# Householder steps of a 64x64 eigensolver beside a graph layer: explicit reflector products in place of a replicated rank-two update

## The chip, the cores and the metric

The kernel runs on one core of one Trainium2 chip. The metric is the device time of one execution in microseconds (us). A comparison is made from the medians of several runs; the profile shows one execution.

## The reference

Four graph layers follow each other, each ending in `x = layernorm(x + layer(x))`, over `x` of 128 batches, 64 nodes and 256 features, with one 64x64 matrix `adj`. All is float32.

```python
# layer 0
def slconv(x, adj, S, W):
    return einsum('nm,bmh->bnh', adj * S, einsum('bnf,fh->bnh', x, W))   # S is adj here
h = relu(slconv(x, adj, adj, W1)); h = relu(slconv(h, adj, adj, W2)); out = slconv(h, adj, adj, W3)

# layer 1
deg = sum(A, 0) + sum(A, 1) - diagonal(A); d = where(deg > 0, rsqrt(deg), 0)
_, U = eigh(d[:, None] * (diag(deg) - A) * d[None, :])
h = relu(einsum('mn,bnd->bmd', U.T, x) @ W1 + b1); out = einsum('nm,bmd->bnd', U, h @ W2 + b2)

# layer 2: two graph convolutions, then four LSTMs over windows of 1 to 4 nodes
# layer 3: x @ W + b_lin, scores masked by adj, softmax over the 64 nodes, sum of neighbours
```

What matters here is that layer 1 needs the eigenvectors `U` of a 64x64 matrix that depends on `adj` alone. So they can be computed while layer 0 runs.

## The kernel before

**Part one** is layer 0 together with the eigenvectors. The 8192 rows (batch times node) lie in `X` as 64 tiles of 128 rows. `layer0(g)` takes two tiles, for g from 0 to 31: mixing over nodes with `sqT2` (the squared, transposed matrix of two batches on the diagonal), the product with `aw1`, ReLU, mixing, the product with `aw2`, ReLU, the product with `aw3`, mixing, then an addition to `X` on VectorE (L626) and `rows_norm`, whose statistics run on VectorE, whose power runs on GpSimd (L452, L453) and whose last step runs on VectorE (L455). ScalarE moves the results from PSUM, as ReLU (L584) or copy (L595, L622). Five PSUM buffers (`psa`) serve layer 0.

`eigen()` computes the eigenvectors in these stages: the normalised Laplacian; 62 Householder steps to a tridiagonal matrix, which also collect the transformation in `QT`; the eigenvalues by six passes of a bisection with 16 points each (L272 to L289, VectorE alone); the eigenvectors of the tridiagonal matrix by recurrences from both ends (L302 to L304) and a choice of signs; then `U` and its transpose for two batches, `u2` and `ut2`. `eigen()` has three PSUM tags of one buffer each: `pa`, `pb`, `pc`. All its products go through one helper (L75), and all products of layer 0 and later go through another (L576), so their lines in the profile are these two; the tile names tell the products apart.

**The Householder step before.** The matrix and `QT` stand side by side in one tile `AQ` of 128 partitions, of which the upper 64 are zero in their constants. A step has two products, issued one after the other. The first, with the vector `v` broadcast as weights, gives `v` times the matrix and `v` times `QT` in all 128 partitions; the second fetches the next row, by a unit vector. Everything else is some 24 small VectorE instructions on rows and columns: the length of the vector, one square root on ScalarE (L145), the coefficients, and the rank-two update of `AQ` in place (L174 to L176).

**What sets the order.** Inside part one TensorE's instructions are recorded by hand. `layer0(g)` and `eigen()` are generators. Each `yield` returns the estimated time at which its next products may be issued; a loop at the end of part one picks `eigen()` if it is due, else the first of two running layer-0 groups. The clock `now` is advanced by stated costs: in layer 0 by `2 * max(0.0009 * columns, 0.112)` us per product, in `eigen()` by 0.2 us. `eigen()` states its own due times with

```python
    def after(n, turns=0):
        clock[0] += 0.21 * n + 0.6 * turns
        return clock[0] + 0.3
```

where `n` counts VectorE instructions. The other engines' orders are set by the framework's scheduler. Every engine works off its queue in order, so a TensorE product that waits for VectorE holds up all products behind it.

**Part two** is layers 1 to 3, over 16 groups of four tiles, three at a time, with an order of its own. Layer 1 needs `u2` and `ut2`, and starts when layer 0's last group is through. The change does not touch it.

Of the kernel before, what the change touches and what calls it, by code (L numbers as in the profile page):

```python
# [10 lines left out]
F32 = mybir.dt.float32  # L11
AF = mybir.ActivationFunctionType
ALU = mybir.AluOpType
AX = mybir.AxisListType

N = 64
FAN = 16
PASSES = 6
CONSTS = ["eye", "rev", "sup", "sub", "ones", "off", "idx"]


def constants():
    k = np.arange(N)
    eye = np.eye(N)
    sup = np.eye(N, k=1)
    c = {
        "eye": eye,
        "ones": np.ones((N, N)),
        "rev": eye[::-1],
        "sup": sup,  # L30
        "sub": sup.T,
        "off": 1 - eye,
        "idx": np.tile(k, (N, 1)),
    }
    out = np.zeros((2 * N, len(CONSTS), N), np.float32)
    out[:N] = np.stack([c[n] for n in CONSTS], axis=1)
    return out


def eigen(tc, stack, a, cst, u2, ut2, now):  # L40
# [9 lines left out]
    V, S, PE = nc.vector, nc.scalar, nc.tensor  # L50
    cp = stack.enter_context(tc.tile_pool(name="ec", bufs=1))
# [4 lines left out]
    def sb(shape, tag):  # L56
        uid[0] += 1
        return wp.tile(shape, F32, tag=tag, name=f"{tag}_{uid[0]}")

    def ps(shape, tag):  # L60
        uid[0] += 1
        return pp.tile(shape, F32, tag=tag, name=f"{tag}_{uid[0]}")

    W = 2 * N
    C = {n: cst[:N, i, :] for i, n in enumerate(CONSTS)}
    eye = cst[:, CONSTS.index("eye"), :]
    clock = [now[0]]

    def after(n, turns=0):

        clock[0] += 0.21 * n + 0.6 * turns
        return clock[0] + 0.3

    def mm(out, lhsT, rhs):
        PE.matmul(out, lhsT, rhs, start=True, stop=True)  # L75
        now[0] += 0.2
        clock[0] = now[0] + 0.5

    def rowdot(out, x, y):
        junk = sb([N, N], "junk")  # L80
        V.scalar_tensor_tensor(junk, x, 1.0, y, op0=ALU.mult, op1=ALU.mult, accum_out=out)


    aT = ps([N, N], "pa")
    PE.transpose(aT, a, C["eye"])
    s2 = sb([N, N], "s2")
    V.tensor_add(s2, a, aT)
    dia = sb([N, 1], "c0")
    rowdot(dia, a, C["eye"])
    deg = sb([N, 1], "c1")  # L90
# [6 lines left out]
    y = sb([N, 1], "c4")  # L97
# [11 lines left out]
    V.tensor_scalar(m, s2, -0.5, None, op0=ALU.mult)  # L109
    V.tensor_mul(m, m, C["off"])  # L110
    V.scalar_tensor_tensor(m, C["eye"], dl, m, op0=ALU.mult, op1=ALU.add)
    dm = sb([N, N], "dm")
    V.tensor_scalar(dm, C["eye"], y, None, op0=ALU.mult)
    pm = ps([N, N], "pa")
    yield after(20, 1)
    mm(pm, m, dm)

    AQ = cp.tile([W, 2, N], F32, name="AQ")
    V.memset(AQ[:, 0, :], 0.0)
    V.tensor_copy(AQ[:, 1, :], eye)  # L120
    V.tensor_scalar(AQ[:N, 0, :], pm, y, None, op0=ALU.mult)
    A, QT = AQ[:N, 0, :], AQ[:N, 1, :]
    yield after(3)

    pq = ps([W, 3, N], "pc")
    mm(pq[:, 2, :], eye[:, 0:1].to_broadcast([W, W]), AQ[:, 0, :])  # L130
    xr = sb([W, N], "xr")
    V.tensor_copy(xr, pq[:, 2, :])
    after(1)
    for i in range(N - 2):
        j = i + 1
        q = sb([W, 16], "q")
        rest, rm, ss, sq, g0, sg, rc, n2, vv, th, s0, c2, qi = (q[:, k:k + 1] for k in range(13))
        u = sb([W, 4], "u")
        v, vt, pt, qt = (u[:, k:k + 1] for k in range(4))
        v0 = xr[:, j:j + 1]  # L140
        V.scalar_tensor_tensor(sb([W, N], "junk")[:, j + 1:], xr[:, j + 1:], 1.0, xr[:, j + 1:], op0=ALU.mult,
                               op1=ALU.mult, accum_out=rest)
        V.tensor_scalar(rm, rest, 1e-30, None, op0=ALU.add)
        V.tensor_scalar(ss, v0, v0, rm, op0=ALU.mult, op1=ALU.add)
        S.activation(sq, ss, AF.Sqrt)  # L145
        V.tensor_scalar(g0, rest, 0.0, -1.0, op0=ALU.is_gt, op1=ALU.mult)
        V.tensor_scalar(sg, v0, 0.0, 0.5, op0=ALU.is_ge, op1=ALU.subtract)
        V.reciprocal(rc, sq)
        V.tensor_scalar(n2, ss, rc, sq, op0=ALU.mult, op1=ALU.add)
        V.scalar_tensor_tensor(v0, n2, sg, v0, op0=ALU.mult, op1=ALU.add)  # L150
        V.scalar_tensor_tensor(sb([W, N], "junk")[:, j:], xr[:, j:], 1.0, eye[:, j:], op0=ALU.mult, op1=ALU.mult,
                               accum_out=v)
        yield after(21, 0.5)
        pq = ps([W, 3, N], "pc")
        mm(pq[:, 0:2, :], v.to_broadcast([W, W]), AQ)
        mm(pq[:, 2, :], eye[:, j:j + 1].to_broadcast([W, W]), AQ[:, 0, :])
        V.tensor_scalar(vv, v0, v0, rm, op0=ALU.mult, op1=ALU.add)
        V.reciprocal(vv, vv)
        V.tensor_mul(th, vv, g0)
        V.tensor_scalar(s0, v0, th, 2.0, op0=ALU.mult, op1=ALU.mult)  # L160
        V.tensor_scalar(vt, v, th, 2.0, op0=ALU.mult, op1=ALU.mult)
        V.scalar_tensor_tensor(sb([W, N], "junk")[:, j:], AQ[:, 0, j:], 1.0, xr[:, j:], op0=ALU.mult, op1=ALU.mult,
                               accum_out=pt)
        V.tensor_scalar(pt, pt, th, 2.0, op0=ALU.mult, op1=ALU.mult)
        V.scalar_tensor_tensor(sb([W, N], "junk")[:, j:], pq[:, 0, j:], th, xr[:, j:], op0=ALU.mult, op1=ALU.mult,
                               accum_out=c2)
        qr = sb([W, N], "qr")
        V.scalar_tensor_tensor(qr[:, j:], xr[:, j:], c2, pq[:, 0, j:], op0=ALU.mult, op1=ALU.add)
        V.tensor_scalar(qi, qr[:, j:j + 1], th, 2.0, op0=ALU.mult, op1=ALU.mult)
        nx = sb([W, N], "xr")  # L170
        V.scalar_tensor_tensor(nx[:, j + 1:], qr[:, j + 1:], s0, pq[:, 2, j + 1:], op0=ALU.mult, op1=ALU.add)
        V.scalar_tensor_tensor(nx[:, j + 1:], xr[:, j + 1:], qi, nx[:, j + 1:], op0=ALU.mult, op1=ALU.add)
        V.scalar_tensor_tensor(qt, vt, c2, pt, op0=ALU.mult, op1=ALU.add)
        V.scalar_tensor_tensor(AQ[:, 0, j:], qr[:, j:], vt, AQ[:, 0, j:], op0=ALU.mult, op1=ALU.add)  # L174
        V.scalar_tensor_tensor(AQ[:, 0, j:], xr[:, j:], qt, AQ[:, 0, j:], op0=ALU.mult, op1=ALU.add)
        V.scalar_tensor_tensor(AQ[:, 1, :], pq[:, 1, :], vt, AQ[:, 1, :], op0=ALU.mult, op1=ALU.add)  # L176
        xr = nx


    de = cp.tile([N, 4], F32, name="de")  # L180
    d, e, ep, g = (de[:, j:j + 1] for j in range(4))
    rowdot(d, A, C["eye"])
    rowdot(e, A, C["sup"])
# [19 lines left out]
    def rows(col, n, tag):  # L203
        b = sb([N, N], "bc")
        V.tensor_scalar(b, C["ones"], col, None, op0=ALU.mult)
        yield after(5)
        p = ps([N, n, N], tag)
        mm(p, b, cst[:N, 0:n, :])
        return p

    co = cp.tile([N, 20], F32, name="co")
# [13 lines left out]
    t0, t1, t2, big, ae, sg = w_[11:17]  # L225
# [45 lines left out]
    for _ in range(PASSES):  # L271
        V.tensor_scalar(h, h, 1.0 / (FAN + 1), None, op0=ALU.mult)  # L272
        x = sb([N, FAN], "bx")
# [3 lines left out]
        for k in range(1, N):  # L277
# [3 lines left out]
            if k % 2:  # L281
                yield after(5)
        V.scalar_tensor_tensor(M.rearrange("p j k -> p k j"), Q, 0.0, inb.unsqueeze(2).to_broadcast([N, N, FAN]),
                               op0=ALU.is_lt, op1=ALU.mult)
# [3 lines left out]
                               accum_out=co_[6])  # L288
# [10 lines left out]
    for k in range(1, N):  # L299
        c = N - 1 - k  # L300
# [35 lines left out]
    Z = cp.tile([N, N], F32, name="Z")  # L336
# [76 lines left out]

    yield after(16)
    pu = ps([N, N], "pa")
    mm(pu, Z, QT)
    UT = cp.tile([N, N], F32, name="UT")
    V.tensor_scalar(UT, pu, co_[12], None, op0=ALU.mult)
    yield after(1)
    pt = ps([N, N], "pb")  # L420
# [15 lines left out]
P = 128  # L436
# [23 lines left out]
def kernel(  # L460
# [26 lines left out]
    V, S, PE = nc.vector, nc.scalar, nc.tensor  # L487
# [5 lines left out]
    def tl(pool, shape, tag):  # L493
        uid[0] += 1
        return pool.tile(shape, F32, tag=tag, name=f"{tag}_{uid[0]}")
# [7 lines left out]
    pa = phase_a.enter_context(tc.tile_pool(name="pa", bufs=2))  # L503
    ea = phase_a.enter_context(tc.tile_pool(name="ea", bufs=1))
# [9 lines left out]
    nc.gpsimd.memset(ad2, 0.0)  # L514
    adst = keep.tile([P, N], F32, name="adst")
    a64 = ea.tile([N, N], F32, name="a64")
    eig_c = ea.tile([P, len(CONSTS), N], F32, name="eig_c")
    nc.sync.dma_start(a64, adj)
    for h in range(2):
        hs = slice(h * N, (h + 1) * N)  # L520
# [19 lines left out]
    ones = keep.tile([P, P], F32, name="ones")  # L540
# [26 lines left out]
    pt = tl(psa, [P, 512], "ps")  # L567
# [7 lines left out]
    def mm(out, lhsT, rhs, start=True, stop=True):  # L575
        PE.matmul(out, lhsT, rhs, start=start, stop=stop)  # L576
        now[0] += 2 * max(0.0009 * rhs.free_size(), 0.112)
# [52 lines left out]

    todo = [layer0(g) for g in range(NT // 2)]
    eig = [0.0, eigen(tc, phase_a, a64, eig_c, u2, ut2, now)]
    going = []
    with tc.manual_schedule(engines={mybir.EngineType.PE}):
# [18 lines left out]
    pr = tl(psa, [P, 512], "ps")  # L653
# [13 lines left out]
    pg = ctx.enter_context(tc.tile_pool(name="pg", bufs=WAYS, reuse_waits="tile"))  # L667
    pw = ctx.enter_context(tc.tile_pool(name="pw", bufs=5, reuse_waits="tile"))
    pv = ctx.enter_context(tc.tile_pool(name="pv", bufs=4, reuse_waits="tile"))
# [314 lines left out]
```

## Time and profile before

| what | value |
|---|---|
| median of three runs | 2722.86 us (2721.37 to 2723.87) |
| the profiled execution | 2722.86 us, its span 2721.1 us |
| busy TensorE, VectorE, ScalarE, GpSimd over the span | 95%, 49%, 38%, 9% |
| first to last Householder product (pc tiles) | 25.50 to 385.31 us |
| last product ahead of the bisection | 396.89 us |
| first product behind the bisection and the recurrences (L335) | 701.19 us |
| last products of `eigen()` | 727.72 us |
| last product of layer 0 | 982.50 us |
| mean granted TensorE clock | 0.983 of full speed |

In the profile PE is TensorE's products, PEld its weight loads, DVE is VectorE, ACT ScalarE, POOL GpSimd, SP the queue that issues most transfers. A row of a timeline gives the start in us, the duration, the engine, the line, the operation, output and inputs by tile name, then shapes. For PE "64*64" is the size of the weights, and what follows it is output partitions times columns. One float32 product leaves two records. Records of PE overlap, since products are pipelined; what a product costs is therefore read from the starts of its neighbours, not from its own duration. In brackets stands the idle time ahead of a row, and what ended it.

### The profile page before, as it was taken

The numbers are of one execution on the slowest core, as the hardware profiler recorded it, in microseconds if no ns is written. First come the engines' busy times: TensorE is split into PE (matmuls) and PEld (weight loads), VectorE is DVE, ScalarE is ACT, GpSimd is POOL, SyncE is SP. The second block draws the span as 40 slices with busy tenths as digits, with TensorE's granted clock in tenths as the row PEclk, the third lists the DMA queues.
The fourth block names the chain that finished last, engine by engine and source line by source line (L and its number), as shares of the span: only waits on it lengthen the run. The fifth ranks groups of instructions, "written<-read, shape, count | busy, mean of one in ns | idle before, by whom it ended". The sixth has DMA issues, their size and how long they took to land.

```text
span 2721.1 us, 39771 instructions
## 1 busy us (share of the span) xinstructions
PE 2593.5 (95%) x15384; PEld 2256.5 (83%) x15384; DVE 1334.8 (49%) x5277; ACT 1029.7 (38%) x2525; POOL 239.8 (9%) x336
## 2 busy tenths in 40 slices
PE   7999999999899989999999999999999999999995
PEld 6888877777688878898898898898898988978993
DVE  5777768888401033444444434445444444442335
ACT  2222222222122224544444544544444444445442
POOL 0000000000000020111101101101101101110012
PEclk9999999999899999999999999999999999999996
DMA  8000000000000010000000000000000000000000
GB/s 267 1 1 1 1 1 1 1 1 1 1 1 0 1 47 1 1 9 9 9 1 8 4 6 9 1 9 9 1 9 9 1 9 9 1 9 1 1 1 24
DMA packets 24398, 32.19 MB, mean 12 GB/s; under 512 B 2336, under 2 KB 21024, under 8 KB 24208
## 3 DMA queue, kind: packets, MB, share of 16 engines
q1 hardware_dynamic: 24032, 29.19, 3.2%
q8 instruction: 121, 1.98, 0.3%
q0 software_dynamic: 176, 0.46, 0.1%
q14 instruction: 69, 0.57, 0.1%
HBM read 21.25 MB, written 8.39 MB: 11 GB/s over the span
## 4 chain that ended last, share of the span: by engine, by line
PE 48%; DVE 4%; ACT 3%; POOL 2%; issue 1%; POOLq 0%; DVEq 0%; ACTq 0%
PE ps L576 47%; PE ps L683 1%; POOL ln_rs L453 1%; DVE X L455 1%; ACT gates L782 1%; DVE X L911 1%; ACT L887 1%; ACT L782 1%; DVE X L845 1%; PE ps L874 1%; DVE ln_st L450 1%; ACT att L887 0%; POOL ln_rs L452 0%; ACT gates L790 0%; DVE ln_mv L451 0%
## 5 line engine op out<-in xcount | busy, mean ns | idle before, releaser
L576 PE MATMUL ps<-w,wih 128*128 128x128 f32 (+2 forms) x4992 | 894.1, 319 | 3.5 <-DVE w L801 3.5
L576 PEld LDWEIGHTS ps<-w,wih 128*128 128x128 f32 x4992 | 763.8, 191 | 51.6 <-issue 10.1
L782 ACT ACTIVATE gates<-ps,cbi 128x128 f32<-128x128 f32 (+2 forms) x1248 | 500.4, 410 | 549.7 <-PE ps L576 542.1
L576 PE MATMUL ps<-hs,whh 128*128 128x128 f32 (+2 forms) x3072 | 537.5, 303 | 0.0
L576 PEld LDWEIGHTS ps<-hs,whh 128*128 128x128 f32 x3072 | 454.8, 191 | 24.9 <-issue 10.5
L576 PE MATMUL ps<-m,aw 128*128 128x256 f32 x2048 | 456.4, 381 | 2.1 <-DVE tw L303 2.1
L576 PEld LDWEIGHTS ps<-m,aw 128*128 128x128 f32 x2048 | 386.2, 190 | 64.2 <-issue 11.4
L584 ACT ACTIVATE h<-ps 128x256 f32<-128x256 f32 (+1 forms) x320 | 136.5, 426 | 445.3 <-PE ps L576 445.3
L576 PE MATMUL ps<-aw,h 128*128 128x256 f32 x1024 | 228.9, 380 | 0.0
L576 PEld LDWEIGHTS ps<-aw,h 128*128 128x128 f32 x1024 | 193.2, 190 | 36.7 <-issue 12.2
L787 DVE TENSOR_TENSOR gates<-gates 128x256 f32<-128x256 f32 (+2 forms) x256 | 92.6, 362 | 221.8 <-ACT gates L782 221.4
L452 POOL TENSOR_SCALAR ln_rs<-ln_mv 128x2 f32<-128x2 f32 x128 | 29.6, 231 | 1447.6 <-DVE ln_mv L451 1245.6
L455 DVE TENSOR_SCALAR X<-X,ln_mv,ln_rs 128x256 f32<-128x256 f32 x256 | 100.9, 433 | 107.2 <-POOL ln_rs L453 107.1
L790 ACT ACTIVATE gates<-c 128x128 f32<-128x128 f32 (+2 forms) x288 | 98.1, 341 | 96.1 <-DVE c L789 84.7
L801 DVE TENSOR_TENSOR w<-gates 128x256 f32<-128x256 f32 (+2 forms) x160 | 61.7, 395 | 147.7 <-PE ps L576 109.2
L626 DVE TENSOR_TENSOR X<-ps,X 128x512 f32<-128x512 f32 x32 | 21.8, 681 | 225.7 <-PE ps L576 225.7
L576 PE MATMUL ps<-aw,m 128*128 128x512 f32 x256 | 128.7, 628 | 0.0
L786 DVE TENSOR_TENSOR c<-c,gates 128x128 f32<-128x128 f32 (+2 forms) x192 | 63.8, 332 | 129.6 <-ACT gates L782 127.3
L792 DVE TENSOR_TENSOR hs<-gates 128x128 f32<-128x128 f32 (+2 forms) x192 | 62.9, 328 | 105.0 <-ACT gates L790 74.6
L837 POOL COPY w<-w 128x512 f32<-128x512 f32 x32 | 35.6, 1119 | 816.0 <-DVE w L801 594.3
L450 DVE BATCH_NORM_STATS2 ln_st<-X 128x6 f32<-128x256 f32 x256 | 99.5, 409 | 1.3
L279 DVE RECIPROCAL br<-Q 64x16 f32<-64x16 f32 x378 | 92.3, 244 | 12.2
(324 smaller groups left out, 2658.8 us busy)
## 6 DMA issues: line engine op xcount, KB each, us to landing
X<-in_x_dram SPq DMA_DIRECT2D x32, 256.0 KB, 6.2
out_dram<-X SPq DMA_DIRECT2D x32, 256.0 KB, 2.1
wih<-in_c_ih_dram SPq DMA_DIRECT2D x4, 1024.0 KB, 8.3
aw<-in_a_w_dram SPq DMA_DIRECT2D x3, 1024.0 KB, 11.3
whh<-in_c_hh_dram SPq DMA_DIRECT2D x3, 1024.0 KB, 5.5
aw<-in_a_w_dram SPq DMA_DIRECT2D x1, 512.0 KB, 6.7
cw<-in_c_w_dram SPq DMA_DIRECT2D x2, 256.0 KB, 4.0
bw<-in_b_w_dram SPq DMA_DIRECT2D x2, 128.0 KB, 4.2
```

Of the source, the lines that this page charges most:

```text
L279: V.reciprocal(r, Q[:, k - 1, :])
L450: nc.vector.bn_stats(st[:, t, :], x[:, t, :])
L455: nc.vector.tensor_scalar(x[:, t, :], x[:, t, :], mv[:, t, 0:1], rs[:, t:t + 1], op0=ALU.subtract, op1=ALU.mult)
L576: PE.matmul(out, lhsT, rhs, start=start, stop=stop)
L584: S.activation(dst, src, AF.Relu)
L782: S.activation(gate[q][:, h, :], pp, AF.Tanh if q == "g" else AF.Sigmoid, bias=bias[:, j:j + 1])
L786: V.tensor_mul(c[:, h, :], c[:, h, :], gate["f"][:, h, :])
L787: V.tensor_mul(to, gate["i"][:, h, :], gate["g"][:, h, :])
L790: S.activation(gate["i"][:, h, :], c[:, h, :] if p > 1 else to, AF.Tanh)
L792: V.tensor_mul(new[:, h, :], gate["o"][:, h, :], gate["i"][:, h, :])
L801: V.tensor_mul(hT[:, h, slice(first + p - 1, first + nw * p, p), :], gate["o"][:, h, :].rearrange("p (w b) -> p w b", b=8), gate["i"][:, h ...
L837: nc.gpsimd.tensor_copy(as3(hb[:, k, :], 8), hT[:, k, :, :].rearrange("p n b -> p b n"))
```

## The change

The change was recorded under the name "Layer 0 and the eigenvectors: the kernel orders TensorE's products itself from stated latencies; loads reordered; later pools reuse bytes tile by tile", in place of "Own order of TensorE for layer 0". The diff itself touches only `eigen()` and its constants. The tile `AQ` goes. The matrix `A`, the transformation `QT` and the reflector `H` are 64x64 tiles of 64 partitions. A step now has five products. `R` (a sum over partitions by a matrix of ones, for two columns) gives the length. `dv` (a diagonal matrix times ones) spreads `v` over the partitions. `H = I - 2 v v'/(v'v)` is then formed, and applied as `B = A H`, `H QT` and `A = H B`. VectorE copies `A` and `B` from PSUM, ScalarE copies `QT`. There are four yields in a step instead of one. The constants become a tile of 64 partitions with eight matrices instead of 128 partitions with seven.

```diff
-CONSTS = ["eye", "rev", "sup", "sub", "ones", "off", "idx"]
+CONSTS = ["eye", "rev", "sup", "sub", "ones", "low", "off", "idx"]
...
-    pq = ps([W, 3, N], "pc")
-    mm(pq[:, 2, :], eye[:, 0:1].to_broadcast([W, W]), AQ[:, 0, :])
-    xr = sb([W, N], "xr")
-    V.tensor_copy(xr, pq[:, 2, :])
     for i in range(N - 2):
-        j = i + 1
...
-        V.scalar_tensor_tensor(sb([W, N], "junk")[:, j + 1:], xr[:, j + 1:], 1.0, xr[:, j + 1:], op0=ALU.mult,
-                               op1=ALU.mult, accum_out=rest)
-        V.tensor_scalar(rm, rest, 1e-30, None, op0=ALU.add)
-        V.tensor_scalar(ss, v0, v0, rm, op0=ALU.mult, op1=ALU.add)
-        S.activation(sq, ss, AF.Sqrt)
...
-        yield after(21, 0.5)
-        pq = ps([W, 3, N], "pc")
-        mm(pq[:, 0:2, :], v.to_broadcast([W, W]), AQ)
-        mm(pq[:, 2, :], eye[:, j:j + 1].to_broadcast([W, W]), AQ[:, 0, :])
...
-        V.scalar_tensor_tensor(AQ[:, 0, j:], qr[:, j:], vt, AQ[:, 0, j:], op0=ALU.mult, op1=ALU.add)
-        V.scalar_tensor_tensor(AQ[:, 0, j:], xr[:, j:], qt, AQ[:, 0, j:], op0=ALU.mult, op1=ALU.add)
-        V.scalar_tensor_tensor(AQ[:, 1, :], pq[:, 1, :], vt, AQ[:, 1, :], op0=ALU.mult, op1=ALU.add)
-        xr = nx
+        R = sb([N, 4], "R")
+        x, xt = R[:, 2:3], R[:, 3:4]
+        V.tensor_mul(x, A[:, i:i + 1], C["low"][:, i:i + 1])
+        V.tensor_mul(xt, A[:, i:i + 1], C["low"][:, i + 1:i + 2])
+        V.tensor_mul(R[:, 0:1], xt, xt)
+        V.tensor_sub(R[:, 1:2], x, xt)
+        yield after(4)
+        pr = ps([N, 2], "pc")
+        mm(pr, C["ones"], R[:, 0:2])
+        q = sb([N, 10], "q")
+        V.tensor_copy(q[:, 0:2], pr)
...
+        V.tensor_scalar(ss, al, al, rest, op0=ALU.mult, op1=ALU.add)
+        V.tensor_scalar(ss, ss, 1e-30, None, op0=ALU.max)
+        S.activation(q[:, 3:4], ss, AF.Sqrt)
...
+        V.scalar_tensor_tensor(v, C["eye"][:, i + 1:i + 2], v0, xt, op0=ALU.mult, op1=ALU.add)
+        dv = sb([N, N], "dv")
+        V.tensor_scalar(dv, C["eye"], v, None, op0=ALU.mult)
+        yield after(9, 1)
+        pv = ps([N, N], "pa")
+        mm(pv, C["ones"], dv)
...
+        V.tensor_scalar(tv, v, q[:, 9:10], q[:, 8:9], op0=ALU.mult, op1=ALU.mult)
+        H = sb([N, N], "H")
+        V.scalar_tensor_tensor(H, pv, tv, C["eye"], op0=ALU.mult, op1=ALU.add)
+        yield after(2)
+        ph = ps([N, 2, N], "pb")
+        pg = ps([N, N], "pa")
+        mm(pg, A, H)
+        mm(ph[:, 1, :], H, QT)
+        B = sb([N, N], "B")
+        V.tensor_copy(B, pg)
+        yield after(1)
+        mm(ph[:, 0, :], H, B)
+        A = sb([N, N], "A")
+        V.tensor_copy(A, ph[:, 0, :])
+        QT = sb([N, N], "QT")
+        S.copy(QT, ph[:, 1, :])
+        after(1)
...
-    eig_c = ea.tile([P, len(CONSTS), N], F32, name="eig_c")
+    eig_c = ea.tile([N, len(CONSTS), N], F32, name="eig_c")
```

## The prediction

> **What bounds the kernel now.** I read the table of stretches first, because busy shares over the whole span mix stages. Its columns are length, then busy time of PE, PEld, DVE, ACT and POOL with their instructions, then the granted clock.
>
> ```profile
> 26.00:385.00 359.00, 358.20 (x1799) 299.84 (x1799) 270.02 (x1869) 93.90 (x265) 10.33 (x23) 1.00 0.09 31
> 397.00:701.00 304.00, 273.58 (x1244) 222.87 (x1244) 264.81 (x1135) 66.07 (x160) 8.35 (x18) 0.96 0.00 1
> 728.00:975.00 247.00, 247.00 (x1162) 204.09 (x1161) 22.37 (x66) 61.54 (x150) 8.34 (x18) 1.00 0.00 1
> ```
>
> The first row is layer 0 beside the 62 Householder steps: PE is busy 358.2 of 359 us. The second is layer 0 beside the bisection: PE idles 30 us, and the clock is 0.96. The third is layer 0 alone; eigen() has ended at 728. The next view, the waits of PE from 26 to 385 us, has this one row:
>
> ```profile
> PE pc L75 <- DVE junk L151: 0.8, 2, 0.5
> ```
>
> So the eigenvectors' DVE chain is hidden in this stretch; only its TensorE products cost time. Over the whole first part (0 to 990 us) the waits that matter are
>
> ```profile
> PE ps L576 <- DVE X L626: 17.6, 4, 5.7
> PE pa L335 <- DVE w L331: 11.0, 1, 11.0
> PE ps L576 <- DVE tw L303: 2.1, 1, 2.1
> ```
>
> all in the bisection, where DVE is the limit. What a product costs is read from the timeline of PE, as spacing of the layer-0 records around it. Start and duration come first; a float32 product is two records.
>
> ```profile
> 189.93 0.38 PE L75 MATMUL pc<-AQ,u 128*128 128x128 f32 x2
> 190.15 0.33 PE L75 MATMUL pc<-AQ,eig_c 128*128 128x64 f32 x2
> ...
> 195.55 0.39 PE L75 MATMUL pc<-AQ,u 128*128 128x128 f32 x2
> ```
>
> ```profile
> 392.69 1.99 PE L576 MATMUL ps<-m,aw 128*128 128x256 f32 x8
> 394.61 0.43 PE L75 MATMUL pb<-eig_c,bc 64*64 64x128 f32 x2
> 394.97 1.99 PE L576 MATMUL ps<-m,aw 128*128 128x256 f32 x8
> ...
> 717.18 5.45 PE L576 MATMUL ps<-m,aw 128*128 128x256 f32 x24
> 722.55 0.33 PE L75 MATMUL pa<-AQ,Z 64*64 64x64 f32 x2
> 722.81 1.99 PE L576 MATMUL ps<-m,aw 128*128 128x256 f32 x8
> ```
>
> The unit is one 128x256 record of layer 0: 64 in a row run from 960.89 to 974.70, so 0.2158 us each. A 512-column record counts two, a 128-column one half. From 189.93 to 195.55 lie 24 units (5.18 us), which leaves **0.44 us for the two products of a step together**. From 717.18 to 722.81 lie 24 units again, in 5.63 us, with one 64*64 product: **0.45 us for one**. 713.27 to 717.18 gives 0.46 (16 units, one product). With 128 columns it is 0.55 (2.28 less 1.73), and with one column 0.30 (390.66 to 392.69, 2.03 less 1.73). A 64*64 product between 128*128 ones thus costs twice what its columns would. In the timeline of weight loads the reason is visible: the load of a 64*64 product begins with its MATMUL, after "0.33 <-issue", while that of a 128*128 one begins 0.21 us ahead (189.72 for 189.93).
>
> **What the Trainium skill says.** "TensorEngine Tiling (Array Packing)", Key Properties: "Changing tiling mode (not just tile) drains the TensorE". The trace agrees, with the 0.45 against 0.22 us above. "TensorE: Matmul & The Clock Gate", the two states of the HAM clock gate: an idle window of about 3.4 us halves the clock until activity returns. The trace agrees: after the 11.0 us wait the stretch 701.2 to 712 has clock 0.74. Gaps of 0.25 us are far below that.
>
> **The change part by part.**
>
> The diff touches eigen() and its constants only. From the first product of layer 1 on, PE's order of instructions is the same, and nothing on SP's or POOL's queue moves past anything. Loads and pools, which the change's given name mentions, do not change.
>
> *Products.* A step had two products with 128*128 weights, back to back. It gets five with 64*64 weights, in four places with layer-0 work between them in the order that the build fixes (62 of each): R with 2 columns, dv, the pair AH and HQT, and HB. Prices: R 0.30 (the one-column row), dv 0.45, HB 0.45. The pair is not shown anywhere: the second needs no switch, so it costs its columns, 0.22 (half of the 0.44), at least nothing if it hides behind the first, at most 0.45 if it switches again; I take 0.45 + 0.22 = 0.67. Sum 1.87 per step against 0.44, so 1.43 more; times 62 is **88.9 us**. One product ahead of the loop (L132's, 0.22) goes: 88.7. If the switch cost nothing here: 5 x 0.22 - 0.44 = 0.66, or 41 us. If the pair's second product hid: 1.21, or 75 us; if it cost a switch of its own: 1.66, or 103 us.
>
> *How much of it is on the path.* All, if PE stays the limit. In the recorded orders, layer 0 is 4096 units in both. Beside the Householder steps lie 1536 before, 2508 after; beside the bisection 1224 in both, with nine X updates in both; behind it 1272 before, 296 after. The first figure can be tested: 1536 x 0.2158 + 62 x 0.44 = 358.8 us, and the trace has 359.8 from the first to the last pc product (25.50 to 385.31). After: 2508 x 0.2158 + 62 x 1.87 = 657 us, so the steps end at about 683 instead of 385. The bisection takes 304 us again: 1224 units are 264, the three waits 30.7, and the rest, about 9, is the lower clock. So the idle time there moves but neither grows nor shrinks. The remaining products, 701.19 to 727.72, took 27 us; 296 units are 64 us, so eigen() still ends some 37 us ahead of layer 0. That cover shrinks from 1272 units; if it were gone the tail would add up to 27 us.
>
> *DVE.* A step's rows sum to 5.6 us now and to about 4.2 from like rows (0.15 for a 1-column product, 0.27 with two pointers, 0.22 to 0.28 for 64x64). But PE now waits on DVE at four places, not one. From the start of the R product to that of dv: 0.37 until its reader starts (68.33 to 68.70), copy 0.2, ss 0.3, max to reciprocal over ACT 0.6, then five small rows of 0.2 to 0.3 and 0.15 back to PE, 2.9 us. The order leaves mostly 16 units and a product, 3.45 + 0.3 = 3.8. For dv to the pair it is 1.5 of 2.2; pair to HB 0.8 of 2.4; HB to R 1.6 of 2.2. All fit, with 0.6 to 1.6 spare. What doesn't fit is an X update: its DVE rows, 0.68 + 2 x 0.41 + 2 x 0.17 + 2 x 0.41, are 2.7 us, and 0.8 of waiting for POOL. Behind a late link stands PE's next layer-0 product, and behind that everything. Bounds: zero; or 20 updates x (3.5 - 0.6) = 58 us. In the trace the 12 updates cost 0.8 us in all, since their rows are interleaved with the chain's; I take 2 us.
>
> *Edits that I cost at nothing.* The 62 ACT copies of QT (about 0.25 each, 16 us) lie in 74% idle ACT time; uncovered they are 16 us. Layer 0's relus queue behind them, but five PSUM buffers (some 9 us of products) stand between. The square root stays. The constants load, 224 KB, becomes 128 KB; PE's first product waits for it until 11.0 us. That could shift the start by half a microsecond either way. The bytes of the later pools differ little; no wait for them shows.
>
> *Sum.* 88.7 + 2 = 90.7 on the profiled execution's 2722.86 us (span 2721.1), which is also the median: **2813.5 us**, 3.3% more. What a measurement here can tell from no change is about 0.2%, 5 us.
>
> **The rivals.**
>
> 1. *Products without the switch.* TensorE may keep up when the next 64*64 product is ready long before. Against it: the products at 713 to 723 were ready too (their operands' DVE rows ended microseconds earlier). Gives 2723 + 41 + 2 = 2766. Chance 0.09.
>
> 2. *DVE is late at the four links.* Each X update stalls PE, and some stalls pass the 3.4 us of the clock gate. For it: in the bisection this is what happens (L626, four waits). Against: DVE has 1.4 us less to do per step and slots that are longer by the switches. Gives up to 2723 + 89 + 58 = 2870, half of it 2841. Chance 0.12.
>
> 3. *DVE, not PE, sets the Householder stretch* (the other side). Then its end follows DVE's rows, 5.6 down to 4.2 us per step, and the five products run in idle PE time: 62 x 1.4 = 87 us less, 2636. It decides only if PE idles at least the added 89 us in that stretch; the trace has 0.8 us of waits in 359. Chance 0.02.
>
> 4. *The change moves nothing*: layer 0's waits in the bisection (30.7 and 9) vanish through the other alignment while the products cost 41: 2725. Against: the same 1224 units and nine updates. Chance 0.02.
>
> **How the numbers follow.** The forecast case has 0.75; its own range, with the pair's price open (75 to 103 us) and some us of waits, is 2798 to 2832. To leave out no more than 2 in 10 I reach up to half of rival 2 and down toward rival 1 without including it: 2786 to 2845. Faster has 0.02, within 0.2% 0.02, slower 0.96.
>
> **What would show it.** Right: from about 26 to 680 us PE has no waits of note but its layer-0 records are spaced by 0.45 us at each lone 64*64 product; five products a step; eigen()'s last product near 1026 us, layer 0's end near 1073 instead of 983; the same three waits in the bisection; everything from layer 1 on unchanged in length. Wrong: PE waits for dv, H, B or R adding up to over 10 us, a step's five products costing near 1.1 us, or layer 0 waiting for eigen() at its end.

## The result, and the profile after

The changed kernel takes 2814.76 us in the median of four runs (2814.28 to 2818.87), beside 2722.14 us of the kernel before in the same comparison: 92.6 us more, a ratio of 1.0343 with a 95% interval of 1.0325 to 1.0361. The profiled execution has a span of 2813.2 us, 92.1 more than before.

Line numbers from the middle of `eigen()` on are four lower now: layer 0's products are L572. `eigen()`'s helper is L72, three lower. First the table of stretches of the changed kernel, columns as before: layer 0 beside the Householder steps, beside the bisection, and alone.

```profile
26.00:692.00 666.00, 662.05 (x3184) 487.60 (x3183) 265.52 (x1445) 163.98 (x461) 17.77 (x38) 1.00 0.05 17
700.00:1007.00 307.00, 275.04 (x1255) 223.24 (x1254) 266.70 (x1141) 68.60 (x167) 9.32 (x20) 0.96 0.00 1
1033.00:1077.00 44.00, 43.27 (x200) 36.56 (x200) 3.10 (x10) 8.51 (x21) 2.38 (x5) 1.00 0.14 50
```

The first stretch has nearly doubled, and PE is busy in all but 4 us of it. VectorE's share there has fallen from 75% to 40%. The second is nearly as it was; the third has shrunk from 247 us to 44. The waits of PE in the first part:

```profile
PE ps L572 <- DVE X L622: 19.8, 4, 5.5
PE pa L331 <- DVE w L327: 11.6, 1, 11.6
PE pa L72 <- DVE q L151: 3.1, 5, 0.6
PE ps L572 <- DVE tw L299: 0.9, 1, 0.9
PE pa L72 <- DVE H L157: 0.5, 2, 0.3
```

The three waits of the bisection are back (19.8, 11.6 and 0.9 us, beside 17.6, 11.0 and 2.1). The waits of the steps themselves are the third and the last row, 3.6 us in 62 steps. (The row named L151 runs right beside that of `dv`; the wait is for `dv`.) One step on PE, from the timeline:

```profile
300.59 1.99 PE L572 MATMUL ps<-m,aw 128*128 128x256 f32 x8
302.51 0.32 PE L72 MATMUL pa<-H,A 64*64 64x64 f32 x2
302.68 0.28 PE L72 MATMUL pb<-QT,H 64*64 64x64 f32 x2
302.89 1.99 PE L572 MATMUL ps<-m,aw 128*128 128x256 f32 x8
304.81 0.32 PE L72 MATMUL pb<-B,H 64*64 64x64 f32 x2
305.07 1.99 PE L572 MATMUL ps<-m,aw 128*128 128x256 f32 x8
306.99 0.27 PE L72 MATMUL pc<-R,eig_c 64*64 64x2 f32 x2
307.19 3.72 PE L572 MATMUL ps<-m,aw 128*128 128x256 f32 x16
310.84 0.32 PE L72 MATMUL pa<-dv,eig_c 64*64 64x64 f32 x2
311.10 1.99 PE L572 MATMUL ps<-m,aw 128*128 128x256 f32 x8
```

A place is a spot in TensorE's order with layer-0 products on either side. The price of each place is the distance between two layer-0 rows less the layer-0 records between (8 are 1.73 us, 16 are 3.45): the pair 2.30 - 1.73 = 0.57, H B 0.45, R 2.12 - 1.73 = 0.39, dv 3.91 - 3.45 = 0.46. Together they are **1.88 us** a step.

Where the 92.1 us of the span come from, from the same marks in both timelines:

| from, to | before | after | difference |
|---|---|---|---|
| start to the product of `dm`, the last ahead of the steps | 23.42 | 25.53 | +2.1 |
| to the first product behind the steps | 365.25 | 666.39 | +301.1 |
| to the last product ahead of the bisection | 8.22 | 8.25 | 0.0 |
| to the first product behind it (L335, now L331) | 304.30 | 307.14 | +2.8 |
| to the first product behind layer 0 | 282.27 | 69.79 | -212.5 |
| to the end | 1737.6 | 1736.1 | -1.5 |

Of the 301.1 us, 976 units of layer 0 that have moved there from behind the bisection are 210.6; what is left, 90.5 us, is the step's own growth, waits included. The last row is the same code in every run. It takes 1735.8 to 1740.6 us in the traces of this study (but for f2 below, where layer 1 waits for `eigen()`): so much single executions differ.

### The profile page after: what moved, and what is told of

Same layout as the page of the kernel before. It is cut to its first block, busy times and chain, and to the rows that moved or that the text cites. A ratio compares the mean times of both kernels' runs of the same rounds, so it can differ in the third digit from the quotient of the medians.

```text
span 2813.2 us, 40127 instructions
## 1 busy us (share of the span) xinstructions
PE 2680.4 (95%) x15754; PEld 2265.3 (81%) x15754; DVE 1309.8 (47%) x4780; ACT 1043.0 (37%) x2587; POOL 239.3 (9%) x336
## 4 chain that ended last, share of the span: by engine, by line
PE 47%; DVE 4%; ACT 3%; POOL 2%; issue 1%; POOLq 0%; DVEq 0%; ACTq 0%
PE ps L572 45%; PE ps L679 1%; POOL ln_rs L449 1%; DVE X L451 1%; ACT gates L778 1%; DVE X L907 1%; ACT L883 1%; ACT L778 1%; PE ps L870 1%; DVE X L841 1%; DVE ln_st L446 1%; ACT att L883 0%; POOL ln_rs L448 0%; ACT gates L786 0%; DVE ln_mv L447 0%
## 5 line engine op out<-in xcount | busy, mean ns | idle before, releaser
L572 PE MATMUL ps<-w,wih 128*128 128x128 f32 (+2 forms) x4992 | 894.9, 319 | 3.5 <-DVE w L797 3.5
L572 PEld LDWEIGHTS ps<-w,wih 128*128 128x128 f32 x4992 | 764.2, 191 | 51.7 <-issue 10.1
L572 PE MATMUL ps<-hs,whh 128*128 128x128 f32 (+2 forms) x3072 | 536.1, 303 | 0.0
L572 PE MATMUL ps<-m,aw 128*128 128x256 f32 x2048 | 481.6, 387 | 0.9 <-DVE tw L299 0.9
L572 PEld LDWEIGHTS ps<-hs,whh 128*128 128x128 f32 x3072 | 453.6, 191 | 24.4 <-issue 10.5
L572 PEld LDWEIGHTS ps<-m,aw 128*128 128x128 f32 x2048 | 379.2, 190 | 61.2 <-issue 6.5
L572 PE MATMUL ps<-aw,h 128*128 128x256 f32 x1024 | 241.0, 385 | 0.0
L572 PEld LDWEIGHTS ps<-aw,h 128*128 128x128 f32 x1024 | 189.1, 190 | 32.9 <-issue 7.2
L783 DVE TENSOR_TENSOR gates<-gates 128x256 f32<-128x256 f32 (+2 forms) x256 | 92.6, 362 | 220.8 <-ACT gates L778 220.4
L572 PE MATMUL ps<-aw,m 128*128 128x512 f32 x256 | 130.8, 636 | 0.0
L591 ACT COPY m<-ps 128x256 f32<-128x256 f32 x192 | 71.3, 372 | 67.9 <-PE ps L572 58.9
```

Source lines behind the costliest of these rows:

```text
L591: S.copy(dst[:, c, :], p[:, :2 * P])
L783: V.tensor_mul(to, gate["i"][:, h, :], gate["g"][:, h, :])
```

## The experiments

Each comparison ran the kernel before beside it; its medians there were 2725.7, 2726.1 and 2725.7 us. So differences are given to the kernel before of the same comparison: for the changed kernel that is +92.6 us. The changed kernel itself was not run again there. "More than the changed kernel" below is thus the difference of two such differences, with some 6 us of uncertainty from their two intervals; where a few us matter, the timelines decide.

**No change of the array's size** (e1). The products' operands live in tiles of 128 partitions, zero outside the 64x64 part.

```diff
-        pr = ps([N, 2], "pc")
-        mm(pr, C["ones"], R[:, 0:2])
+        pr = ps([W, 2], "pc")
+        mm(pr, on, wR[:, 0:2])                       # on: 128x128 ones
...
-        mm(pg, A, H)
-        mm(ph[:, 1, :], H, QT)
+        mm(pg, wA, wH[:, :N])                        # wA, wH: 128x128, wQ: 128x64
+        mm(ph[:, 1, :], wH, wQ)
```

> The changed kernel with the same five products per step, but with the operands padded with zeros to 128 partitions and 128 weight columns, so that no product changes the size of the array in use; order, counts and the VectorE rows stay. Theory (each place where 64*64 products stand between 128*128 ones costs a drain): the five products cost 5 x 0.22 = 1.1 us a step instead of the 1.88 that the changed kernel's trace shows, 62 x 0.78 = 48 us less than the changed kernel's 2815: 2767 us, and the weight loads of these products start ahead of their MATMUL again. Rival (a small lone product is dear because it waits for VectorE or stands alone, whatever its size): no change, 2815 us.

Measured: 2777.6 us, +51.9, ratio 1.0188 (1.0172 to 1.0203); so 41 us of the 92.6 are gone. In the timelines, the stretch from `dm` to the first product behind the steps is 622.9 us instead of 666.4: 43.5 less, 0.70 a step. The weight loads of PE show it; first the changed kernel, then this one:

```profile
304.81 0.19 PEld L72 LDWEIGHTS pb<-B,H 64*64 64x64 f32 x2 [0.33 <-issue]
305.06 1.59 PEld L572 LDWEIGHTS ps<-m,aw 128*128 128x128 f32 x8
```

```profile
307.02 0.41 PEld L72 LDWEIGHTS pb<-wB,wH 128*128 128x128 f32 x2
307.35 1.60 PEld L586 LDWEIGHTS ps<-aw,h 128*128 128x128 f32 x8
```

The 64*64 load starts at 304.81 together with its MATMUL, after 0.33 us in which nothing is loaded. The full-size one starts at 307.02, and its MATMUL follows at 307.23: the load lies under the product ahead. The rival, that a small lone product is dear because it waits, gave 2815 and is out. Both the partitions and the weight columns were padded; which of the two matters was not tested. The saving in the timelines is 0.08 us a step short of the forecast. Waits in the steps, 5.5 us instead of 3.6, are 0.03 of it; the rest stays open.

**The same products in five places** (e2). H QT leaves the pair and goes out alone, behind the next step's R.

```diff
+        due = after(9, 1)
+        if hq is not None:
+            yield now[0] + 0.3
+            PE.matmul(hph[:, 1, :], hH, QT, start=True, stop=True)     # H and ph of the step before
...
+        yield due
-        mm(ph[:, 1, :], H, QT)
```

> The changed kernel with the product H QT taken out of the pair and issued alone, one place later, between the R and the dv product of the next step; the same five products, now in five places. Theory (places are paid, not products): as the pair's second it cost 0.574 - 0.457 = 0.12 us, alone it costs 0.46, so 62 x 0.34 = 21 us more than the changed kernel: 2836 us. Rival (products are paid, each by its size): 2815 us.

Measured: 2838.9 us, +113.2, ratio 1.0413 (1.0398 to 1.0429); 20.6 us more than the changed kernel, beside 21 forecast. The steps' stretch grows by 21.9 us, of which 1.7 are eight units of layer 0 that moved into it. So a small product that follows another small one costs 0.12, and in a place of its own about 0.33 more.

**One more small product behind the pair, in the kernel before** (e3).

```diff
         mm(pq[:, 2, :], eye[:, j:j + 1].to_broadcast([W, W]), AQ[:, 0, :])
+        PE.matmul(ps([N, N], "pa"), C["ones"], C["eye"], start=True, stop=True)
```

> The kernel before with one more product in every step, 64*64 weights and 64 columns of constants, right behind the step's two; its result is used by nothing. Theory: 62 x 0.46 = 28 us more, 2750 us. Rival (only the columns count, 0.11 to 0.22 us): 7 to 14 us more, 2729 to 2736 us.

Measured: +20.9 us, ratio 1.0076 (1.0061 to 1.0091), 0.34 us a product, with 0.27 to 0.40 from the interval: between the two forecasts, and neither holds. In the timelines the steps' stretch grows from 365.2 to 388.8 us, 0.38 a product.

**One more product in a place of its own, small and full-size** (g1, g2). Both stand between layer-0 products, one place behind the step's pair.

```diff
-        yield after(21, 0.5)
+        due = after(21, 0.5)
+        yield now[0] + 0.3
+        PE.matmul(ps([N, N], "pa"), C["ones"], C["eye"], start=True, stop=True)                # g1
+        PE.matmul(ps([W, N], "pa"), eye[:, 0:1].to_broadcast([W, W]), eye, start=True, stop=True)   # g2
+        yield due
```

> The kernel before with one more 64*64 product of constants in every step, alone between layer-0 products one place behind the step's two (behind them it cost 0.34 us). Theory: there it costs the full 0.46 us that single rows of the trace before showed, 62 x 0.46 = 28 us more, ratio 1.0105; behind the pair it was cheaper because the record ahead of it was a short one. Rival (its price is 0.34 us wherever it stands, and 0.46 was an accident of few rows): 21 us, ratio 1.0077.

> The same place, but the product of constants has 128*128 weights and 64 columns. Theory (no change of the array's size, so only its columns and its two records): 62 x 0.22 = 14 us more, ratio 1.005; the difference between the two is the change of size. Rival (standing alone is what costs): as with the small one.

Measured: g1 +27.1 us, ratio 1.0101 (1.0085 to 1.0118), 0.44 a product; g2 +13.7, ratio 1.0051 (1.0037 to 1.0066), 0.22 a product. Both are as the theory had them. The timelines, g1 first:

```profile
303.26 1.95 PE L579 MATMUL ps<-m,aw 128*128 128x256 f32 x8
305.14 0.33 PE L155 MATMUL pa<-eig_c 64*64 64x64 f32 x2
305.40 1.98 PE L579 MATMUL ps<-aw,m 128*128 128x512 f32 x4
```

```profile
299.39 1.95 PE L579 MATMUL ps<-aw,h 128*128 128x256 f32 x8
301.17 0.33 PE L155 MATMUL pa<-eig_c 128*128 128x64 f32 x2
301.34 3.67 PE L579 MATMUL ps<-aw,h 128*128 128x256 f32 x16
```

Both first rows stand right behind the step's pair, and eight records are 1.73 us. In g2 the extra product starts 0.05 us later than that (1.78) and is followed after 0.17. In g1 it starts 0.15 later (1.88) and is followed after 0.26, although its weights are a quarter of the size and both operands are constants. So the small product starts 0.10 later than the full-size one and takes 0.09 longer to the next row. A last part falls into the row behind: eight records take 1.89 us behind 256-column ones, 1.95 behind a full-size 64-column product (as behind the pair), and 1.99 behind a small one.

This also gives the lower price in e3:

```profile
104.81 0.33 PE L75 MATMUL pc<-AQ,eig_c 128*128 128x64 f32 x2
105.07 0.32 PE L157 MATMUL pa<-eig_c 64*64 64x64 f32 x2
105.33 5.45 PE L577 MATMUL ps<-m,aw 128*128 128x256 f32 x24
```

The small product starts 0.26 us behind the pair's second where 0.17 would do, so it is 0.09 late, about as in g1, and it is followed after 0.26, as in g1. But of the 0.10 us in the row behind, 0.06 were due to the pair anyway. That leaves 0.39 us for e3, beside 0.45 in g1; the stretches of the steps say 0.38 and 0.44. The change of size costs the same in both places.

**More work for VectorE in one link** (e4, f3). Four more dependent copies of B ahead of H B, and, separately, eight of `dv` ahead of its product.

```diff
-        B = sb([N, N], "B")
-        V.tensor_copy(B, pg)
+        B = pg
+        for k in range(5):                           # e4
+            B, B0 = sb([N, N], "B"), B
+            V.tensor_copy(B, B0)
...
+        for _ in range(8):                           # f3
+            dv, d0 = sb([N, N], "dv"), dv
+            V.tensor_copy(dv, d0)
```

> The changed kernel with four more copies in the chain between the pair and the product H B: B is copied on from buffer to buffer, about 1.0 us more on VectorE in every step, dependent on each other. Theory (TensorE is the limit, this link has some 1.5 us to spare): no change, 2815 us. Rival (VectorE's chain is what the longer steps wait for): 62 x 1.0 = 62 us more, 2877 us.

> The changed kernel with eight more dependent copies of dv ahead of its product, about 1.7 us more on VectorE in the link from the R product to the dv product. Theory (this link has about 1.1 us to spare in the changed kernel's trace: dv done 309.75, its product 310.84): 62 x 0.6 = 37 us more than the changed kernel, ratio 1.046 to 1.050 to the kernel before. Rival (VectorE is hidden wholly, 1.034) or (VectorE sets the step already, 62 x 1.7 = 105 us more, 1.073).

Measured: e4 +98.0 us, ratio 1.0359 (1.0341 to 1.0376), whose interval overlaps the changed kernel's; f3 +153.8, ratio 1.0567 (1.0552 to 1.0581), 61 us more than the changed kernel. The waits of PE, e4 and then f3:

```profile
PE pb L72 <- DVE B L166: 2.9, 3, 1.2
```

```profile
PE pa L72 <- DVE dv L149: 54.0, 59, 3.0
```

In e4 the copies added 0.85 us to the link in every step, and 59 of 62 steps did not notice; their stretch in the timelines is 3.2 us longer. In f3 almost every step waits, but not all alike. Two of the 59 waits, in brackets:

```profile
127.08 0.33 PE L72 MATMUL pa<-dv,eig_c 64*64 64x64 f32 x2 [0.58 <-DVE dv L149]
140.74 0.33 PE L72 MATMUL pa<-dv,eig_c 64*64 64x64 f32 x2 [3.00 <-DVE dv L149]
```

47 waits are of 0.5 to 0.7 us, 27.4 us together: that is the forecast of 0.6 a step, with a link that grew by 1.8 us and not 1.7. The other 12 are of 1.5 to 3.0 us, 26.5 together. In those steps the rows of an X update of layer 0 stand in VectorE's queue between the R product and the copies of `dv`. The expectation had left them out, and they are most of why f3 lost 61 us and not 37. So VectorE's chain is hidden with about 1 us of reserve in this link, and a link that grows by more brings on what rival 2 of the prediction asked for: waits in every step, the longest at X updates.

**The idle time of the bisection** (f1, f6), in the kernel before: a later due time at the end of each pass, and then a sixth PSUM buffer for layer 0 as well.

```diff
         V.tensor_scalar(lo, co_[6], h, lo, op0=ALU.mult, op1=ALU.add)
-        yield after(20)
+        yield after(45)                              # f1 and f6
...
-    psa = ...tile_pool(name="psa", bufs=5, ...)
+    psa = ...tile_pool(name="psa", bufs=6, ...)      # f6, and tag "pb" becomes "pc" in eigen()
```

> The kernel before with one number changed: at the end of each of the six bisection passes eigen() states 45 VectorE instructions ahead of its next product instead of 20. TensorE gets 1360 units of layer 0 beside the bisection instead of 1224; nothing else moves. Theory (in the prediction, that idle time in the bisection is set by VectorE and by where the order puts the product at L335): the wait at L335 (11 us) and the half-speed stretch behind it (about 3 us) go, the waits for X updates (17.6 us) stay: 14 us less, ratio 0.995. Rival (VectorE sets the stretch, so the idle time only moves into longer waits for X updates): no change.

> The same later due time, and eigen() uses two PSUM tags instead of three, so that layer 0 has six PSUM buffers instead of five. Theory: each of the four waits for an X update shrinks by the products of one more buffer, some 1.7 us[...]: another 7 to 15 us less, ratio 0.990 to 0.992. Rival: the waits stay, since VectorE is late by more than a buffer each time: as with the later due time alone.

Measured: f1 -3.8 us, ratio 0.9987 (0.9981 to 0.9994); f6 -4.9 us, ratio 0.9981 (0.9974 to 0.9988). The waits, f1 and then f6:

```profile
PE ps L576 <- DVE X L626: 25.2, 6, 6.1
```

```profile
PE ps L576 <- DVE X L626: 24.2, 6, 5.9
```

The wait at L335 is gone from both, but the waits for X updates grow from 17.6 us (four) to 25.2 (six). The rival is nearly right: VectorE limits this stretch, and most of what PE no longer waits for at the end it waits for on the way. The other part of the theory, the slow stretch behind L335, came true: from the product at L335 to `eigen()`'s last product, 26.6 us became 23.9 with the same layer-0 work between, and the granted clock behind L335 is 1.00 where it was 0.74. f6 is the fastest kernel of the study; its interval overlaps f1's, so what the sixth buffer adds is open.

**The cover gone** (f2), in the changed kernel.

```diff
-        yield after(9, 1)
+        yield after(9, 4)
```

> The changed kernel with one number changed: eigen() states 1.8 us more ahead of the dv product. The order then puts 2988 units of layer 0 beside the Householder steps instead of 2520, 1040 beside the bisection, and none behind it. TensorE's instructions are the same in number. Theory (layer 0 covers the bisection and the tail; its 296 units behind the bisection were the reserve): the steps end 480 x 0.2158 = 104 us later, eigen() ends near 1130 us instead of 1033, and layer 1 starts then instead of at 1077: 50 to 55 us more than the changed kernel, ratio about 1.054. Rival (TensorE's total is what counts, order does not): no change to the changed kernel, 1.034.

Measured: 2848.9 us, +122.8, ratio 1.0452 (1.0437 to 1.0466); 30 us more than the changed kernel, not 50 to 55. The wait of PE that it made:

```profile
PE pa L331 <- DVE w L327: 55.1, 1, 55.1
```

Layer 0 ended at about 1051 us, and layer 1 had to wait for `eigen()`, whose last product came at 1115 instead of 1033. Its tail behind L331 took 9 us, not the 26 that I had carried over. Those 26 were mostly layer-0 products between its own, which were no longer there. That is 17 of the some 23 us that the forecast was too high. Layer 1 also started more smoothly: its first wait for VectorE (`w`, L703), 4.6 us in the changed kernel, is 0.3 here. The direction is as said: with TensorE's products the same in number, order alone cost 30 us.

## Why the prediction was right, step by step

- **The sum.** Forecast 88.7 us of products and 2 of waits, 90.7; measured 92.6. The step cost 1.88 us, forecast 1.87. Two of its terms were off by 0.1 us each and cancelled, so that the sum came this close is in part luck. The pair was put at 0.67 and costs 0.57, because the second small product adds 0.12 and not its columns' 0.22; e2 shows the same from the other side. R was put at 0.30, from the row with one column, and costs 0.39. That reading was too short, as shown below this list. A slip of 0.2 us stands in the sum too: 62 x 1.43 is 88.7, and less 0.2 for L132's product 88.4.
- **The switch of size.** It was read from a handful of rows in the trace before, and "the reason" from the weight loads. g1 against g2 prices it at 27.1 - 13.7 = 13.4 us for 62 products, 0.22 us each, and e1 takes 43.5 us out of the steps' stretch in the timelines. So rival 1, products without the switch at 2766, is near what padding brings (about 2774 on the chip of the first comparison), not the change. What happens inside TensorE at the switch, and whether the late weight load is its cause or goes along with it, no run separates.
- **VectorE.** Forecast 2 us of waits, within bounds of 0 to 58; measured 3.6. The X updates stayed hidden, but for waits of up to 0.6 us. e4 shows the reserve, f3 its end. Rival 3, VectorE as the limit of the steps, is out: VectorE's busy time fell from 270 us in 359 to 266 in 666, and the stretch nearly doubled.
- **The bisection.** "The idle time there moves but neither grows nor shrinks": 304.3 became 307.1 us. Rival 4 needed it to vanish; f1 shows how little of it goes (1.6 us in that stretch) even when the order is told to fill it.
- **The cover.** `eigen()`'s last product was forecast near 1026 us and came at 1033, layer 0's end near 1073 and came at 1077. The reserve of some 37 us was there (44 us of layer 0 alone). The bound that I gave for its loss, up to 27 us of tail, was not the right size: f2 shows 9 us of tail and a longer wait for the bisection.
- **The start.** Forecast within 0.5 us, measured 2.1 later. It is not the constants' new shape: with the old tile, e3, f1 and f6 wait 13.2, 12.8 and 12.8 us for it, the changed kernel 12.4, and only the profiled execution of before 11.0. The rest of the way to `dm`, 12.4 us before and 13.2 after, is 11.8 to 13.4 over all traces. About 2 of the 92.1 us in the span are thus the difference between two executions.

The row with one column, from the trace before:

```profile
390.66 1.89 PE L576 MATMUL ps<-m,aw 128*128 128x256 f32 x8
392.48 0.27 PE L75 MATMUL pc<-de,eig_c 64*64 64x1 f32 x2
392.69 1.99 PE L576 MATMUL ps<-m,aw 128*128 128x256 f32 x8
```

The eight records ahead of the small product take 1.89 us, those behind it 1.99. The distance from 390.66 to 392.69 leaves out this last 0.10; with it, one column costs 0.40. The other prices were read between two rows that both stand behind a small product, and hold.

## What to carry to other kernels

When a side computation shares TensorE's queue with a dense stream, count its **places** and not its arithmetic: each small product that stands alone pays for the change of the array's size going in and out. Put small products side by side, or pad them with zeros to the size that the stream uses. The price is read from the spacing of the stream's own records, and the weight loads show where the change takes place. And where another engine's chain is hidden, look for how much more it could take in its shortest link, here about 1 us, and what else stands in its queue there, before relying on it.

## What the runs showed of the hardware that I had not expected

A product with weights of a quarter of the array costs twice what a full-size one with the same columns costs, 0.44 against 0.22 us (g1, g2), when its neighbours are full-size. A second small one behind the first adds only 0.12 us, less than the 0.22 of a full-size one. Of the price, 0.10 us does not fall due at the product but in the row behind it (1.99 us for eight records instead of 1.89), so a distance that ends on the next row reads too low. And a full-size product with only 64 columns leaves 0.06 us in the row behind it as well, which is why the small one is cheaper behind it (0.38 us in e3).
